# Spacing the indirect DMAs of a gated scan with a mixture-of-experts layer by waits on TensorE's products

## The chip, the core and the metric

The kernel runs on one core of a Trainium2 chip. A time is the device time of one execution in microseconds (us). The number to predict is the median over several timed executions, which run without the profiler; the profile is one separate execution with the hardware profiler switched on.

## What is computed

The input x has 16 sequences of 256 tokens with 128 channels, 4096 tokens in all. Two layers follow each other, each with a residual:

```
x = x + layernorm(scan(layernorm(x)))       # gated linear recurrence along each sequence
x = x + layernorm(moe(layernorm(x)))        # 32 experts, 4 of them for each token

scan:  i = sigmoid(x Wi + bi);  r = sigmoid(x Wr + br)
       a = exp(-8 softplus(cap) r);  h_t = a_t h_(t-1) + sqrt(1 - a_t^2) i_t x_t
moe:   s = sigmoid(x gate_w^T);  the 4 highest of s + e_bias, weights s normalised over the 4
       out = sum over the 4 of  w * ( (silu(x w1[e]) * (x w3[e])) w2[e] )       # 128 -> 96 -> 128
```

The reference computes all 32 experts for every token and multiplies the unchosen ones by zero.

## The kernel before

The 4096 tokens are cut into eight chunks of 512 tokens. For every chunk, `mix(c)` does the scan layer, the second layernorm and the router. After that a chunk goes one of two ways.

**Two dense chunks (0 and 7).** All 32 experts are computed for all of their tokens, in 24 steps per chunk. A step (`dense`) is two products into the hidden width (`dg` and `du`, line 990), a product that spreads the router weights (`dw`, line 990), an activation (line 998), two multiplications on VectorE (lines 1001 and 1007), and a product that accumulates the output (`acc`, line 1011). These steps depend on no DMA once the weights are in, so they can be run wherever TensorE has nothing else to do.

**Six routed chunks, in two groups (1, 2, 3) and (4, 5, 6).** Their tokens are sorted by expert through DRAM:

1. `send` writes each token's row into `rows_in`, at a place within its expert's rows: 16 indirect DMAs per chunk (4 row tiles of 128 tokens by 4 choices), issued by GpSimd (POOL), line 450.
2. `loads` reads blocks of 128 rows of one expert back (`xb`, line 790), after all 48 sends of the group. SyncE (SP) issues them.
3. `experts` works on tiles of four such blocks, 20 tiles per group: transposes, the `gu` products (line 820), silu and a multiplication, transposes, and the `y_ps` products (line 850). The result goes to `rows_out` in DRAM (line 861).
4. `fetch` reads each token's four results back, 16 indirect DMAs per chunk, line 928, after all the stores of the group. VectorE weighs and adds them (lines 936, 940, 944).
5. `combine` does the last layernorm and the residual and stores the chunk.

POOL issues 192 indirect DMAs and, after the first 20 us, nothing else.

**The order of the work** is not left to queues. The kernel has a planner, the class `Order`, which runs while the program is built. Every piece of work (`mix`, `send`, `dense` and so on) is a generator that yields steps such as `yield PE, 0.86`: an engine, and the time that the step is taken to need. The planner keeps the time at which each engine comes free, always takes the step that can begin first, and among steps of one engine that can begin within 0.3 us of each other the one with the earliest due time. The code behind a `yield` is issued at once when its step is chosen. So the order of the instructions in each engine's queue is the order of the planned beginnings, with all engines interleaved in one sequence. On the chip only data dependences hold, and each engine takes its queue in order. The planned times themselves do not reach the chip.

The planned steps that matter here are a send or fetch of one row tile, `yield POOL, 1.29 * K` (K is 4, so 5.16 us for four DMAs), and those of the products: 0.86 us for `dg`, `du` and `acc`, 0.22 us for `dw`, `0.33 * m` for m blocks of `gu` and `0.22 * nb` for nb blocks of `y_ps`. Dense steps have the latest due times for TensorE (400 and more), so they are taken when nothing else is ready.

Of the kernel before, what the change touches and what calls it, by code (L numbers as in the profile page):

```python
# [18 lines left out]
P = 128  # L19
EPS = 1e-5  # L20
K = 4
GROUPS = ((1, 2, 3), (4, 5, 6))
DENSE = (0, 7)
MIXES = 6
TILES = 40
HELD = 4
# [2 lines left out]
PE, DVE, ACT, POOL, SP, TIME = "pe", "dve", "act", "pool", "sp", "time"  # L29
# [88 lines left out]
SOON = 0.3  # L118
STAY = 6.0
LEAD, STEP, PACE = 45.0, 20.6, 0.9  # L120
SLOT, UNTIL = "slot", "until"


@with_exitstack
def tile_gated_scan_then_moe(
# [28 lines left out]
    nc = tc.nc  # L154
# [6 lines left out]
    SEQS = CH // T  # L161
    NG = len(GROUPS)
    TG = [CH * len(chunks) for chunks in GROUPS]
    UB = E * I // P
    NB = [t * K // P + E - 1 for t in TG]
    NBM = max(NB)
    QB = 4
    RB = 3
    assert C == P and H == P and CH % T == 0 and E * I % P == 0 and 3 * E <= P
    assert sorted(sum(GROUPS, ()) + DENSE) == list(range(N // CH))  # L170

# [20 lines left out]
    def after(ins, others):  # L192

        for o in others:
            tc.add_manual_dep(
                ins.ins, o.ins.name,
                mybir.DependencyInfo(mybir.DependencyClass.Sync, mybir.DependencyReason.DATA),
                reason="rows in DRAM",
            )
# [225 lines left out]
    def apart(ins, key):  # L425

        tc.declare_no_dep(ins.ins, group=key, reason="rows of their own")
        tc.add_to_no_dep_group(key, ins.ins)
# [7 lines left out]
    def normalize(comb, pool, c):  # L436
# [2 lines left out]
        nc.vector.reciprocal(total, total)  # L439
        nc.vector.tensor_tensor(comb, comb, total.to_broadcast([P, TPC, E]), ALU.mult)  # L440

    def send(g, cg):

        c = GROUPS[g][cg]
        yield UNTIL, lambda: times["rows", c][0] if ("rows", c) in times else None
        _, rows, hn = times["rows", c]
        for j in range(TPC):
            yield POOL, 1.29 * K
            for k in range(K):
                ins = nc.gpsimd.indirect_dma_start(  # L450
                    out=rows_in[g],
                    out_offset=bass.IndirectOffsetOnAxis(ap=rows[:, j, k : k + 1], axis=0),
                    in_=hn[:, j, :], in_offset=None,
                )
                apart(ins, f"in_{g}")
                sent[g].append(ins)
        times["sent", g] = order.now
        yield TIME, 2.5
        give("hn", "w")
# [25 lines left out]
    def mix(c):  # L485

        g = next((g for g in range(NG) if c in GROUPS[g]), None)
        if g is not None:
            cg = GROUPS[g].index(c)
        yield UNTIL, lambda: 0.0 if c < MIXES else times.get(("mixed", c - MIXES))  # L490
# [266 lines left out]
    ended = [0] * NG  # L757
# [36 lines left out]
    def experts(g, q):  # L794

        nb, n_ = min(QB, NB[g] - q), f"{g}_{q}"
        yield UNTIL, lambda: times["xb", g, q][0] if ("xb", g, q) in times else None
        yield UNTIL, lambda: 0.0 if began[g] == q // QB else None
        yield SLOT, "blk", "w", "w", "w"
        began[g] += 1  # L800
        _, xb = times["xb", g, q]
        yield SLOT, "s", "ps"
        yield PE, 0.11 * nb
        pt = bank(f"xT_ps_{n_}")
        for b in range(nb):
            nc.tensor.transpose(pt[:, b * P : (b + 1) * P], xb[:, b, :], ident)  # L806
        give("xb", "w")
        yield ACT, 0.6
        xT = work.tile([P, QB * P], F32, tag="w", name=f"xT_{n_}")
        nc.scalar.copy(xT[:, : nb * P], pt[:, : nb * P])  # L810
        give("s", "ps")
        act = work.tile([P, QB, P], F32, tag="w", name=f"act_{n_}")[:, :, :I]
        for h in range(0, nb, 2):
            m = min(2, nb - h)
            yield SLOT, "s", "ps"
            yield PE, 0.33 * m
            pg = bank(f"gu_{n_}_{h}")[:, : 4 * I].rearrange("p (b f) -> p b f", b=2)
            for b in range(m):
                _, e = regs[g, q + h + b]
                nc.tensor.matmul(  # L820
                    pg[:, b, :], lhsT=xT[:, (h + b) * P : (h + b + 1) * P],
                    rhs=w13[:, :, bass.ds(e, 1), :].rearrange("h s o i -> h s (o i)"),
                    start=True, stop=True,
                )
            yield ACT, 0.33, "silu"
            nc.scalar.activation(act[:, h : h + m, :], pg[:, :m, 0:I], AF.Silu)  # L826
            yield DVE, 0.35
            nc.vector.tensor_tensor(  # L828
                act[:, h : h + m, :], act[:, h : h + m, :], pg[:, :m, I : 2 * I], ALU.mult
            )  # L830
            give("s", "ps")
        yield SLOT, "s", "ps"
        yield PE, 0.11 * nb
        pa = bank(f"aT_ps_{n_}")
        for b in range(nb):
            nc.tensor.transpose(pa[:I, b * P : (b + 1) * P], act[:, b, :], ident)  # L836
        aT = work.tile([P, QB * P], F32, tag="w", name=f"aT_{n_}")[:I]
        if q // QB % 2:
            yield DVE, 0.6
            nc.vector.tensor_copy(aT[:, : nb * P], pa[:I, : nb * P])  # L840
        else:
            yield ACT, 0.6
            nc.scalar.copy(aT[:, : nb * P], pa[:I, : nb * P])  # L843
        give("s", "ps")
        yield SLOT, "s", "ps"
        yield PE, 0.22 * nb
        py = bank(f"y_ps_{n_}").rearrange("p (b h) -> p b h", h=H)
        for b in range(nb):
            _, e = regs[g, q + b]
            nc.tensor.matmul(  # L850
                py[:, b, :], lhsT=aT[:, b * P : (b + 1) * P],
                rhs=w2_sb[:, bass.ds(e, 1), :].rearrange("i o h -> i (o h)"),
                start=True, stop=True,
            )
        yield SLOT, "yb", "w"
        yield ACT, 0.6
        yb = work.tile([P, QB, H], F32, tag="w", name=f"yb_{n_}")
        nc.scalar.copy(yb[:, :nb, :], py[:, :nb, :])  # L858
        give("s", "ps", "blk", "w", "w", "w")
        yield SP, 0.4  # L860
        done[g].append(nc.sync.dma_start(
            out=rows_out[g].rearrange("(i p) h -> p i h", p=P)[:, q : q + nb, :],
            in_=yb[:, :nb, :],
        ))
        ended[g] += 1
        if (q // QB + 1) % RB == 0 or q + QB >= NB[g]:
            give("regs")
        times["done", g] = order.now
        yield TIME, 2.5
        give("yb", "w")  # L870
# [46 lines left out]
    def fetch(g, cg, j):  # L917

        c = GROUPS[g][cg]
        yield UNTIL, lambda: times["done", g] + 2.5 if ended[g] * QB >= NB[g] else None  # L920
        yield UNTIL, lambda: times["slots", c][0] if ("slots", c) in times else None
        yield UNTIL, lambda: 0.0 if fetched[0] == turn[c] * TPC + j else None
        yield SLOT, "yk", "w"
        _, rows, wk = times["slots", c]
        yield POOL, 1.29 * K
        yk = work.tile([P, K, H], F32, tag="w", name=f"yk_{c}_{j}")
        for k in range(K):
            ins = nc.gpsimd.indirect_dma_start(  # L928
                out=yk[:, k, :], out_offset=None, in_=rows_out[g],
                in_offset=bass.IndirectOffsetOnAxis(ap=rows[:, j, k : k + 1], axis=0),  # L930
            )
            after(ins, done[g])
        fetched[0] += 1
        yield TIME, 2.4
        yield DVE, 0.7
        nc.vector.tensor_tensor(
            yk, yk, wk[:, j, :].unsqueeze(2).to_broadcast([P, K, H]), ALU.mult
        )
        yield DVE, 0.7
        nc.vector.tensor_tensor(yk[:, 0:2, :], yk[:, 0:2, :], yk[:, 2:4, :], ALU.add)  # L940
        yield UNTIL, lambda: times["res", c][0] if ("res", c) in times else None
        yield DVE, 0.4
        ff = times["res", c][1]
        nc.vector.tensor_tensor(ff[:, j, :], yk[:, 0, :], yk[:, 1, :], ALU.add)
        give("yk", "w")
        summed[c] = summed.get(c, 0) + 1
        times["summed", c] = order.now
# [19 lines left out]
    accs, acts = {}, {}  # L967
    downs = [0] * len(DENSE)

    def dense(d, k):  # L970

        c = DENSE[d]
        yield UNTIL, lambda: times["hT", c][0] if ("hT", c) in times else None
# [13 lines left out]

        def product(name, lhsT, rhs):
            ps = bank(f"d{name}_{c}_{k}")
            nc.tensor.matmul(ps, lhsT=lhsT, rhs=rhs, start=True, stop=True)  # L990
            return ps

        yield PE, 0.86
# [24 lines left out]
    def finish(d):  # L1018

        c = DENSE[d]  # L1020
        yield UNTIL, lambda: times["down", d] if downs[d] == UB else None
# [31 lines left out]
    for g, chunks in enumerate(GROUPS):  # L1053
# [15 lines left out]
        ]  # L1069
    for d, c in enumerate(DENSE):  # L1070
        pieces += [
# [36 lines left out]
```

## Time and profile before

| | |
|---|---|
| timed executions | 440.73 us median of 3 (436.21 to 441.47) |
| profiled execution | 580.8 us, of which the span from first to last instruction is 579.1 us |
| mean granted TensorE clock in the profile | 0.823 |
| TensorE (PE) busy | 368.5 us, 64% of the span |
| VectorE (DVE) busy | 313.5 us, 54% |
| ScalarE (ACT) busy | 251.6 us, 43% |
| GpSimd (POOL) busy | 202.9 us, 35% |
| sends (line 450) | 96 indirect DMAs, 92.7 us busy, 965 ns each |
| fetches (line 928) | 96 indirect DMAs, 93.1 us busy, 970 ns each |
| first send, last send begins | 78.62 us, 293.99 us |
| first fetch, first fetch of the second group, last fetch begins | 331.98 us, 463.43 us, 522.52 us |

A row of the timeline gives the start, the duration, the engine, the line, the operation and the tiles, then in brackets the idle time of the engine before the row and what ended it. PEld is the loading of weights into TensorE. "remote" and "another core or an unknown queue" stand where the trace shows no event that ended a wait; "issue" is time in which the engine waited for nothing that the trace shows. The profiled execution took 580.8 us and the timed ones 440.73 us, so a time read from the profile is not on the scale of the timed runs, and a reader has to say each time which of the two is meant.

### The profile page before, as it was taken

What the parts mean: (1) busy time and instruction counts of PE and PEld (TensorE: products, weight loads), DVE (VectorE), ACT (ScalarE), POOL (GpSimd) and SP (SyncE); (2) the same over time, 40 slices, a digit from 0 to 9 for tenths busy, and PEclk for the clock granted to TensorE, in tenths of its full rate; (3) what the DMA queues carried; (4) which work ended last, traced back from release to release, by engine and by line L of the source; (5) the groups of instructions that cost most, each with busy time, mean ns of one, the idle gap of its engine ahead of it and who ended that gap; (6) DMA issues with size and microseconds to landing.
All of it is one profiled execution on the core that took longest, in us unless ns stands there. A gap on an engine that the chain in (4) does not pass through costs nothing.

```text
span 579.1 us, 6527 instructions
## 1 busy us (share of the span) xinstructions
PE 368.5 (64%) x1555; PEld 236.8 (41%) x1555; DVE 313.5 (54%) x1185; ACT 251.6 (43%) x473; POOL 202.9 (35%) x227
## 2 busy tenths in 40 slices
PE   0345766767883982588559863288799993235940
PEld 0123342332432871477447542266678631012410
DVE  6956692839482763287218640257577451013785
ACT  1599895659421741666235311144355520001321
POOL 9200046643645017100720077236400077771000
PEclk9986767779698887699759985599899998666995
DMA  8245535100131133223222432044544212110001
GB/s 236 66 133 140 139 91 152 41 32 25 50 100 64 55 101 100 73 70 109 91 70 59 119 109 71 25 120 132 146 118 139 88 45 54 53 51 14 18 1 54
DMA packets 82068, 48.57 MB, mean 84 GB/s; under 512 B 15696, under 2 KB 78960, under 8 KB 82032
## 3 DMA queue, kind: packets, MB, share of 16 engines
q1 hardware_dynamic: 74976, 35.40, 21.6%
q0 software_dynamic: 6144, 12.60, 7.5%
q10 hardware_dynamic: 912, 0.17, 0.2%
q8 instruction: 13, 0.21, 0.1%
q14 instruction: 23, 0.19, 0.1%
HBM read 25.20 MB, written 22.94 MB: 83 GB/s over the span
## 4 chain that ended last, share of the span: by engine, by line
PE 48%; another core or an unknown queue 16%; DVE 13%; ACT 11%; issue 11%; DMA 1%; ACTq 0%; DVEq 0%
PE gu L820 9%; PE acc L1011 8%; PE y_ps L850 7%; PE dg L990 6%; PE du L990 6%; PE aT_ps L836 3%; PE xT_ps L806 2%; PE pl L569 2%; PE dw L990 1%; PE pi L510 1%; PE pr L510 1%; ACT h L395 1%; DVE nt_a L375 1%; DVE st_a L471 1%
## 5 line engine op out<-in xcount | busy, mean ns | idle before, releaser
L450 POOL DMA_INDIRECT rows_in<-hn,rows x96 | 92.7, 965 | 184.3 <-DVE x_all L551 60.6
L928 POOL DMA_INDIRECT yk<-rows_out,slots x96 | 93.1, 970 | 135.4 <-PE dw L990 50.1
L820 PE MATMUL gu<-w,xT 128*128 x316 | 71.3, 360 | 36.9 <-ACT xT L810 19.0
L1011 PE MATMUL acc<-a,w_all 128*128 128x512 f32 x96 | 58.4, 698 | 48.2 <-DVE a L1007 28.5
L820 PEld LDWEIGHTS gu<-w,xT 128*128 128x128 f32 x316 | 56.8, 210 | 45.9 <-issue 23.3
L998 ACT ACTIVATE a<-dg 128x512 f32<-128x512 f32 x48 | 28.6, 598 | 92.8 <-remote 38.6
L1007 DVE TENSOR_TENSOR a<-a,dw 128x512 f32<-128x512 f32 x48 | 32.4, 684 | 64.3 <-remote 34.9
L850 PE MATMUL y_ps<-w_sb,aT 96*128 x316 | 48.7, 305 | 26.2 <-ACT aT L843 11.3
L828 DVE TENSOR_TENSOR act<-act,gu 128x192 f32<-128x192 f32 x80 | 27.0, 346 | 67.9 <-ACT act L826 53.1
L850 PEld LDWEIGHTS y_ps<-w_sb,aT 96*128 96x128 f32 x316 | 43.8, 212 | 39.9 <-ACT aT L843 16.3
L826 ACT ACTIVATE act<-gu 128x192 f32<-128x192 f32 x80 | 25.7, 330 | 68.7 <-PE gu L820 29.7
L990 PE MATMUL dg<-hT,w 128*128 128x512 f32 x96 | 55.4, 662 | 0.0
L990 PE MATMUL du<-hT,w 128*128 128x512 f32 x96 | 50.9, 612 | 0.0
L858 ACT COPY yb<-y_ps 128x512 f32<-128x512 f32 (+1 forms) x40 | 23.1, 581 | 52.5 <-PE y_ps L850 23.4
L1001 DVE TENSOR_TENSOR a<-a,du 128x512 f32<-128x512 f32 x48 | 32.4, 681 | 23.6 <-issue 7.4
L1011 PEld LDWEIGHTS acc<-a,w_all 128*128 128x128 f32 x96 | 17.0, 211 | 67.9 <-DVE a L1007 40.3
L810 ACT COPY xT<-xT_ps 128x512 f32<-128x512 f32 (+1 forms) x40 | 22.8, 582 | 33.5 <-remote 23.8
L836 PE MATMUL aT_ps<-ident,act 128*96 128x128 f32 x158 | 25.6, 287 | 11.1 <-issue 7.4
L990 PEld LDWEIGHTS dg<-hT,w 128*128 128x128 f32 x96 | 20.2, 217 | 19.0 <-issue 17.6
L836 PEld LDWEIGHTS aT_ps<-ident,act 128*96 128x96 f32 x158 | 18.5, 132 | 19.4 <-issue 15.5
L806 PE MATMUL xT_ps<-ident,xb 128*128 128x128 f32 x158 | 25.4, 297 | 0.4 <-DVE lists L749 0.4
L990 PEld LDWEIGHTS du<-hT,w 128*128 128x128 f32 x96 | 18.7, 205 | 14.6 <-issue 13.0
(205 smaller groups left out, 590.2 us busy)
## 6 DMA issues: line engine op xcount, KB each, us to landing
xb<-rows_in SPq DMA_DIRECT2D x158, 64.0 KB
rows_out<-yb SPq DMA_DIRECT2D x38, 256.0 KB
rows_in<-zeros SPq DMA_DIRECT2D x8, 512.0 KB
w<-in_L_ffn_w_dram SPq DMA_DIRECT2D x8, 384.0 KB
x_all<-in_L_attn_x_dram SPq DMA_DIRECT2D x8, 256.0 KB
w_all<-in_L_ffn_w_dram SPq DMA_DIRECT2D x4, 384.0 KB
w_sb<-in_L_ffn_w_dram SPq DMA_DIRECT2D x4, 384.0 KB
rows_in<-hn,rows POOLq DMA_INDIRECT x96
```

What stands on the lines that cost most here:

```text
L450: ins = nc.gpsimd.indirect_dma_start(out=rows_in[g], out_offset=bass.IndirectOffsetOnAxis(ap=rows[:, j, k : k + 1], axis=0), in_=hn[:, j, ...
L806: nc.tensor.transpose(pt[:, b * P : (b + 1) * P], xb[:, b, :], ident)
L820: nc.tensor.matmul(pg[:, b, :], lhsT=xT[:, (h + b) * P : (h + b + 1) * P], rhs=w13[:, :, bass.ds(e, 1), :].rearrange("h s o i -> h s (o i) ...
L828: nc.vector.tensor_tensor(act[:, h : h + m, :], act[:, h : h + m, :], pg[:, :m, I : 2 * I], ALU.mult)
L836: nc.tensor.transpose(pa[:I, b * P : (b + 1) * P], act[:, b, :], ident)
L850: nc.tensor.matmul(py[:, b, :], lhsT=aT[:, b * P : (b + 1) * P], rhs=w2_sb[:, bass.ds(e, 1), :].rearrange("i o h -> i (o h)"), start=True, ...
L928: ins = nc.gpsimd.indirect_dma_start(out=yk[:, k, :], out_offset=None, in_=rows_out[g], in_offset=bass.IndirectOffsetOnAxis(ap=rows[:, j, ...
L990: nc.tensor.matmul(ps, lhsT=lhsT, rhs=rhs, start=True, stop=True)
L998: nc.scalar.activation(a, pg, AF.Silu)
L1001: nc.vector.tensor_tensor(a, a, pu, ALU.mult)
L1007: nc.vector.tensor_tensor(a, a, pw, ALU.mult)
L1011: nc.tensor.matmul(accs[d], lhsT=w2_all[:, k, :], rhs=a, start=(k == 0), stop=(k == UB - 1))
```

## The change

Three things are changed, all for the indirect DMAs.

- Each send, and each fetch that is issued while `left()` holds, waits for `beat[0]`: the last product that was issued ahead of it in the one planned sequence. Such products are `y_ps` (line 850) of the experts, and `dg`, `du` and `dw` (line 990) of the dense chunks.
- In the planner each indirect DMA has a slot of its own of `RATE`, 1.9 us, where four together had 5.16 us (1.29 us each).
- `left()` is true until both dense chunks have issued all 24 steps and all expert tiles of both groups have ended, in the planned sequence. Fetches issued after that have a slot of 1.26 us and no wait.

```diff
+RATE = 1.9
...
+    beat = [None]
+
+    def in_pace(ins):
+
+        if beat[0] is not None:
+            after(ins, beat)
+
+    def left():
+
+        return sum(downs) < len(DENSE) * UB or any(ended[g] * QB < NB[g] for g in range(NG))
+
     def send(g, cg):
...
         for j in range(TPC):
-            yield POOL, 1.29 * K
             for k in range(K):
+                yield POOL, RATE
                 ins = nc.gpsimd.indirect_dma_start(
...
                 apart(ins, f"in_{g}")
+                in_pace(ins)
                 sent[g].append(ins)
...
-            nc.tensor.matmul(
+            beat[0] = nc.tensor.matmul(
                 py[:, b, :], lhsT=aT[:, b * P : (b + 1) * P],
...
         _, rows, wk = times["slots", c]
-        yield POOL, 1.29 * K
         yk = work.tile([P, K, H], F32, tag="w", name=f"yk_{c}_{j}")
         for k in range(K):
+            yield POOL, RATE if left() else 1.26
             ins = nc.gpsimd.indirect_dma_start(
...
             after(ins, done[g])
+            if left():
+                in_pace(ins)
...
         def product(name, lhsT, rhs):
             ps = bank(f"d{name}_{c}_{k}")
-            nc.tensor.matmul(ps, lhsT=lhsT, rhs=rhs, start=True, stop=True)
+            beat[0] = nc.tensor.matmul(ps, lhsT=lhsT, rhs=rhs, start=True, stop=True)
             return ps
```

`after(ins, others)` adds a dependence: `ins` waits for the semaphores of `others`. `downs[d]` counts the dense steps whose `acc` has been issued, `ended[g]` the expert tiles of a group whose store has been issued. UB is 24, QB is 4 and NB is 79 blocks per group.

More of the change, by code (lines that the diff above doesn't have):

```diff
@@ L21 @@
 K = 4
-GROUPS = ((1, 2, 3), (4, 5, 6))
-DENSE = (0, 7)
+GROUPS = ((1,2,3),(4,5,6))
+DENSE = (0,7)
 MIXES = 6
```

## The prediction

> **What bounds the kernel now.** I read the page first, then the timeline of POOL alone, the timeline of all engines over the last 120 us, the table by stretches, and the chain of waits.
>
> ```profile
> span 579.1 us, 6527 instructions
> ...
> PE 48%; another core or an unknown queue 16%; DVE 13%; ACT 11%; issue 11%; DMA 1%; ACTq 0%; DVEq 0%
> ...
> L450 POOL DMA_INDIRECT rows_in<-hn,rows x96 | 92.7, 965 | 184.3 <-DVE x_all L551 60.6
> L928 POOL DMA_INDIRECT yk<-rows_out,slots x96 | 93.1, 970 | 135.4 <-PE dw L990 50.1
> ```
>
> The chain that ends last runs 48% over PE, but 27% of it (16 + 11, about 153 us of 579.1) is time that no event explains. The timeline of the last stage shows where such time lies:
>
> ```profile
> 468.90 1.12 PE L1011 MATMUL acc<-a,w_all 128*128 128x512 f32 x2
> ...
> 471.89 1.13 PE L1011 MATMUL acc<-a,w_all 128*128 128x512 f32 x2
> ...
> 505.17 0.60 ACT L998 ACTIVATE a<-dg 128x512 f32<-128x512 f32 x1 [18.37 <-remote]
> ...
> 509.31 0.69 DVE L1007 TENSOR_TENSOR a<-a,dw 128x512 f32<-128x512 f32 x1 [13.38 <-remote]
> ...
> 522.52 0.94 POOL L928 DMA_INDIRECT yk<-rows_out,slots  x1 [0.30 <-issue]
> ```
>
> A dense step takes 2.99 us (from one acc to the next) until 480 us. Then ACT sits idle for 18.37 us although its product was ready, while POOL issues fetches 1.25 us apart. By stretches:
>
> ```profile
> 440.00:463.00 23.00, 22.68 (x126) 16.92 (x125) 13.65 (x42) 12.08 (x28) 0.00 (x0) 1.00 0.34 99
> 463.00:480.00 17.00, 15.86 (x38) 5.95 (x37) 9.46 (x16) 2.99 (x5) 12.60 (x14) 1.00 0.17 46
> 480.00:529.00 49.00, 12.88 (x21) 4.89 (x20) 5.51 (x10) 1.79 (x3) 33.11 (x35) 0.64 0.18 48
> 529.00:560.00 31.00, 27.33 (x65) 10.66 (x63) 23.57 (x73) 6.90 (x13) 0.00 (x0) 0.96 0.03 9
> ```
>
> (stretch; length; busy time of PE, PEld, DVE, ACT, POOL; granted clock; DMA share; GB/s.) PE is full before the last run of fetches, 26% busy in the middle of it, full after it. So the profiled run is slowed by whatever stops PE, ACT and DVE some ten DMAs into a run of indirect DMAs, and spacing these DMAs out looks like the cure.
>
> **But the timed runs do not contain most of those stalls.** 580.8 - 440.73 = 140 us is missing from them, and the unexplained part of the chain is 153 us: 13 us would be left. The chain's PE part, 48% or 278 us at a clock of 0.82, may shrink by some 28 us at a fuller clock (0.92, an estimate: the table above has 1.00 outside the runs of fetches), which would leave up to 41 us. So stalls in the timed runs are worth 0 to 41 us; I take near 0, because the last stage alone fits it, as follows. Fetch of the last 48 rows: 463.43 to 523.46, 60.0 us. After it, without stalls: landing about 2 us (estimate from the 2.4 us that the planner leaves), DVE 1.4 us (L936, L940, L944), and from the last layernorm's start at 570.14 to the end 9.0 us: together 12.4 us. Timed: 440.73 - 1.7 (outside the span) - 12.4 - 60.0 = 366.6 us as the start of this run of fetches, against 463.43 in the profile. Of the 140 us, 43 lie behind that point and 97 before it.
>
> What then bounds a timed run is **PE until the experts end at about 364 us, then POOL**: 48 fetches by 1.25 us, solid, while PE does the dense steps left. I count 18 acc pairs after 463 us: 18 x 2.98 = 54 us, hidden in the 60.
>
> [...] The rows of the tile yk:
>
> ```profile
> L928 POOL DMA_INDIRECT yk<-rows_out,slots x96: 939/945/1806, 332.0 to 522.5; - x96
> L936 DVE TENSOR_TENSOR yk<-yk,wk x24: 678/684/748, 373.5 to 568.8; 128x512 f32<-128x512 f32 x24
> ```
>
> Minimum, median and maximum in ns: the multiplication with both inputs in SBUF takes 684 ns inside the runs and outside. All 96 fetches together exceed their median by 93.1 - 96 x 0.945 = 2.4 us. [...]
>
> **The change, part by part.**
>
> *The waits themselves.* 96 sends and at least part of the fetches get a semaphore wait on PE. The nearest row is a waiting instruction on DVE's queue, 21 ns; the spread is 0 to 0.3 us each (the gap that POOL has anyway). I take nothing: POOL is paced by PE, not by this. Nothing but later indirect DMAs is queued behind them on POOL. But SP's loads wait for all sends of a group, with the experts' stores behind them in SP's queue; and DVE's sums (L936 on) wait for fetches, with dense multiplications behind them.
>
> *The sends.* A chunk's 16 sends get 16 x 1.9 = 30.4 us where they had 20.6. Since the products keep the planned order, POOL can no longer run ahead of it. The three chunks of group 0 began at 78.62, 103.75 and 137.52 us and ended at 157.5; taking out the unexplained entries of the chain there (2.6 and 4.1 at 94, 5.1 at 118, 2.2 at 153: 14 us) that is about 143.5. With the slots, back to back: 78.6 + 91.2 = 170. **The experts of group 0 begin 26 us later** (12 if no stall is taken out). PE doesn't have to wait: the dense steps of chunk 0 are there, eight at 2.98 us. DVE, 1.4 us per step beside the routers' work, was the busier engine there; I take five, 15 us. The other 11 us go mostly to the scan work of chunks 5 to 7, drawn forward (some 7 us of PE a chunk, by the share of the first 78 us): 2 us of PE lost, ends 0 and 11. What is late next is group 1: its 48 sends end another 91 us later, while group 0's experts fill PE.
>
> *The fetches of group 0.* 48 x 1.9 = 91 us of slots among expert tiles. There PE is slower than its slots: 8 `y_ps` blocks take 1.16 us against 0.88, `gu` 1.56 against 1.32. At some 1.2 times the slots the fetches take about 109 us, and group 1's experts about 97 (profile: 131 us from 332 to 463, less the 34 of unexplained entries). So POOL comes free up to 12 us after the experts end, in which PE does up to four dense steps; I take the middle, two.
>
> *The dense work is moved.* Five and two steps done earlier leave R = 18 - 7 = 11 behind the start of the last fetches. PE's total is the same, so those fetches start 7 x 2.98 + 2 = **23 us later**, at 389.5.
>
> *The last 48 fetches.* While dense steps are left, a fetch gets 1.9 us of slots, in which a step has 2.8 us (3 x 0.86 + 0.22) and takes 2.98: 2.02 us real. 11 x 2.98 = 32.8 us hold 16.2 fetches; the other 31.8 run at 1.25: 39.8 us. Sum 72.5 against 60.0: **12.5 us more**. Nothing hides it, for this stage is POOL's.
>
> Sum: 23 + 12.5 = +35.4, **476 us timed**. In general it is 53.6 - 1.84 R + L (L is lost PE time): R = 18, L = 0 gives +20; R = 8, L = 11 gives +50. A step moved forward costs, since the work left beside the fetches is what hides them.
>
> *In the profiled execution's own time* the same +35 stands against stalls that should shrink: at 2 us and more between DMAs I guess half to three quarters of the 140, so 580.8 + 35 - 88 = about 528 us. **The profile may become faster while the timed runs become slower.**
>
> **Rivals.**
>
> - *The stalls are in the timed runs* (up to 41 us) and spacing removes them. For it: they hang on back-to-back DMAs. Against it: the 140 us. With R = 18: 440.7 + 20 - 41 = 420. It is 2% faster (432 us) from 29 us of stalls upwards at R = 18, from 44 at R = 11, which is more than the bound. Chance 0.08.
> - *No measurable change* (432 to 450): 25 to 35 us of stalls go and pay for the pace, or the slots do not bind. 445 us, 0.08.
> - *Only the tail pays*: the front delay is covered without dense work (R = 18), 461 us, 0.24. Speaks for it: experts have earlier due times than dense steps and might catch up.
> - *PE starves* between the old and the new start of the experts, and again before group 1: L = 12 to 30, 490 to 505 us, 0.17. Speaks for it: DVE 71% busy in the first 78 us, so dense steps may be too slow to fill.
> - The forecast, 466 to 488 around 476: 0.43.
>
> **How the numbers follow.** Faster 0.08, within 2% 0.08, slower 0.84; 2% is about what a measurement of this kernel can tell from no change (its three runs lie 1.2% apart). The range 450 to 500 leaves out the faster case, most of no change and the far end of starvation. The likeliest case's own range is 466 to 488.
>
> **What would show it.** Right: sends and fetches about 2 us or more apart, released by products of L850 and L990, with 30 us for a chunk; `xb` loads of group 0 later among the dense steps; about 11 acc pairs after group 1's first fetch; that run of 48 fetches over 70 us long; fewer long waits put down to "remote". Wrong: 18 or more acc pairs left there with the fetches still 60 us (the slots do not bind), or a timed median below 440 (the stalls were real). If the timed runs are slower with more stalls in the profile, my reading of the stalls is wrong.

## The result, and the profile after

The timed executions after the change have a median of **478.51 us** (477.88 to 480.04, 4 runs), those of before beside them 439.39 us (436.21 to 441.47, 4 runs). The ratio is 1.090, with a 95% interval of 1.082 to 1.098: the change costs 39 us.

The profiled execution of after took 477.88 us; it is one of these four. From its page, the span, the chain and the two groups of indirect DMAs (count, busy us, mean ns of one, then the idle time of POOL before them and what ended most of it):

```profile
span 476.2 us, 6622 instructions
...
PE 50%; ACT 16%; DVE 14%; issue 10%; POOL 6%; DMA 3%; POOLq 0%; ACTq 0%; SPq 0%; DVEq 0%
...
L462 POOL DMA_INDIRECT rows_in<-hn,rows x96 | 95.4, 994 | 162.5 <-ACT xn L511 61.5
L941 POOL DMA_INDIRECT yk<-rows_out,slots x96 | 93.1, 969 | 95.1 <-PE y_ps L863 20.4
```

Two things are to be seen. The part "another core or an unknown queue", 16% of the chain before, is gone. And a fetch costs POOL what it cost before (969 ns, 970 before); what has changed is when it begins.

The profile shown ahead of the prediction took 580.8 us where timed executions took 440. So the kernel before was profiled again, unchanged. From the page of this second profile:

```profile
span 437.1 us, 6527 instructions
...
PE 58%; ACT 16%; DVE 14%; issue 5%; DMA 3%; POOL 2%; SPq 1%; ACTq 0%; POOLq 0%; DVEq 0%
...
L928 POOL DMA_INDIRECT yk<-rows_out,slots x96 | 94.6, 985 | 83.3 <-PE dw L990 34.0
```

It took 438.82 us and has no such entry. Of the 39 later timed executions of before (434.55 to 442.48 us) none was slow in this way either. All comparisons of traces below are with this second profile.

The first trace is not only slow but incomplete. It holds 5514 updates of semaphores, the second trace of the same kernel 9252, those of all other kernels 9234 to 9356. So it has no landing time for any fetch, where the second one has a median of 2.9 us:

```profile
yk<-rows_out,slots POOLq DMA_INDIRECT x96
```

```profile
yk<-rows_out,slots POOLq DMA_INDIRECT x96, 2.9
```

A wait is called "remote" or put down to an unknown queue where no update is found that ended it. Part of these entries is therefore missing records. The standstill itself is real: all instructions are recorded, and their span is 579.1 us.

**Where the 39 us lie.** The last stage of before by stretches (stretch; length; busy time of PE, PEld, DVE, ACT, POOL; granted clock; DMA share; GB/s), cut where the last 48 fetches begin and where the last dense step ends:

```profile
341.00:364.00 23.00, 22.80 (x126) 16.64 (x124) 13.72 (x43) 11.74 (x27) 0.29 (x1) 1.00 0.32 94
364.00:414.00 50.00, 48.88 (x116) 19.07 (x115) 36.02 (x83) 11.32 (x21) 38.12 (x40) 1.00 0.21 55
414.00:425.00 11.00, 0.66 (x4) 0.42 (x4) 8.91 (x42) 3.52 (x9) 8.46 (x9) 0.60 0.38 97
```

The same of after:

```profile
370.00:393.00 23.00, 22.98 (x119) 16.05 (x118) 13.84 (x30) 9.60 (x21) 11.69 (x13) 1.00 0.41 112
393.00:425.00 32.00, 31.22 (x75) 12.13 (x73) 21.94 (x53) 7.50 (x14) 15.95 (x17) 1.00 0.15 42
425.00:464.00 39.00, 0.90 (x5) 0.42 (x4) 21.53 (x81) 5.38 (x13) 29.83 (x31) 0.57 0.28 73
```

Before, PE still had 50 us of dense work when the last fetches began at 363.71, and 40 of the 48 were issued beside it; POOL went on without PE for 11 us. After, the last fetches begin at 392.91, only 32 us of dense work are left, and only 18 fetches are issued beside it; POOL goes on without it for 39 us. The last fetch is issued 12 us before the end in both. So the 39.1 us between the two spans are

- 29.2 us: the last fetches begin later (363.7 to 392.9), and
- 10.0 us: they take longer (61.2 to 71.2).

The later start splits without remainder, by arithmetic; what causes the two parts is for the experiments to show. It is how much later the last dense step ends (413.7 to 425.2, **11.5 us**: PE time lost) plus how much less dense work is left behind the start (50.0 to 32.3, **17.7 us**: dense work drawn forward). This split is used for every kernel below, each from one profiled execution. The timed executions of before lie up to 8 us apart, so a few us in it can be chance.

### The profile page after: what moved, and what is told of

It reads as the page before. It is cut to its first block, busy times and chain, and to the rows that moved or that the text cites. A ratio compares the mean times of both kernels' runs of the same rounds, so it can differ in the third digit from the quotient of the medians.

```text
span 476.2 us, 6622 instructions
## 1 busy us (share of the span) xinstructions
PE 342.0 (72%) x1555; PEld 220.8 (46%) x1555; DVE 316.2 (66%) x1185; ACT 252.3 (53%) x473; POOL 205.7 (43%) x227
## 4 chain that ended last, share of the span: by engine, by line
PE 50%; ACT 16%; DVE 14%; issue 10%; POOL 6%; DMA 3%; POOLq 0%; ACTq 0%; SPq 0%; DVEq 0%
PE gu L833 10%; PE acc L1026 7%; PE y_ps L863 7%; PE dg L1005 6%; PE du L1005 6%; POOL yk L941 6%; PE aT_ps L849 3%; PE xT_ps L819 3%; DMA yk<-rows_out,slots 2%; ACT h L396 2%; PE dw L1005 2%; ACT hn L396 1%; ACT L542 1%; ACT L534 1%; PE pl L582 1%
## 5 line engine op out<-in xcount | busy, mean ns | idle before, releaser
L462 POOL DMA_INDIRECT rows_in<-hn,rows x96 | 95.4, 994 | 162.5 <-ACT xn L511 61.5
L833 PE MATMUL gu<-w,xT 128*128 x316 | 67.0, 348 | 13.4 <-issue 11.9
L833 PEld LDWEIGHTS gu<-w,xT 128*128 128x128 f32 x316 | 54.4, 202 | 24.1 <-issue 13.7
L1026 PE MATMUL acc<-a,w_all 128*128 128x512 f32 x96 | 53.6, 647 | 7.1 <-DVE a L1022 6.5
L841 DVE TENSOR_TENSOR act<-act,gu 128x192 f32<-128x192 f32 x80 | 26.9, 348 | 43.9 <-ACT act L839 43.7
L1005 PE MATMUL dg<-hT,w 128*128 128x512 f32 x96 | 50.0, 602 | 0.0
L863 PE MATMUL y_ps<-w_sb,aT 96*128 x316 | 43.7, 285 | 3.0 <-ACT act L839 1.0
L863 PEld LDWEIGHTS y_ps<-w_sb,aT 96*128 96x128 f32 x316 | 39.4, 195 | 13.0 <-ACT aT L856 4.2
L1016 DVE TENSOR_TENSOR a<-a,du 128x512 f32<-128x512 f32 x48 | 32.3, 681 | 6.1 <-PE du L1005 3.9
L396 ACT ACTIVATE ff<-ff,sh_d,rs_d 128x128 f32<-128x128 f32 x24 | 9.9, 482 | 36.6 <-DVE sh_d L393 36.6
L849 PE MATMUL aT_ps<-ident,act 128*96 128x128 f32 x158 | 24.4, 281 | 6.0 <-issue 4.7
L951 DVE TENSOR_TENSOR yk<-yk,wk 128x512 f32<-128x512 f32 x24 | 16.5, 688 | 17.4 <-DMA yk<-rows_out,slots 17.3
L1005 PEld LDWEIGHTS du<-hT,w 128*128 128x128 f32 x96 | 17.9, 196 | 17.0 <-issue 12.9
```

The lines of the kernel that those rows point to most:

```text
L462: ins = nc.gpsimd.indirect_dma_start(out=rows_in[g], out_offset=bass.IndirectOffsetOnAxis(ap=rows[:, j, k : k + 1], axis=0), in_=hn[:, j, ...
L833: nc.tensor.matmul(pg[:, b, :], lhsT=xT[:, (h + b) * P : (h + b + 1) * P], rhs=w13[:, :, bass.ds(e, 1), :].rearrange("h s o i -> h s (o i) ...
L841: nc.vector.tensor_tensor(act[:, h : h + m, :], act[:, h : h + m, :], pg[:, :m, I : 2 * I], ALU.mult)
L863: beat[0] = nc.tensor.matmul(py[:, b, :], lhsT=aT[:, b * P : (b + 1) * P], rhs=w2_sb[:, bass.ds(e, 1), :].rearrange("i o h -> i (o h)"), s ...
L1005: beat[0] = nc.tensor.matmul(ps, lhsT=lhsT, rhs=rhs, start=True, stop=True)
L1016: nc.vector.tensor_tensor(a, a, pu, ALU.mult)
```

## The experiments

The first question was what in the 580.8 us belonged to the kernel; then which of the three edits (waits, slots, pace of the last fetches) costs what; then sends against fetches; at last where the lost PE time comes from.

**The kernel before, profiled again** (no edit).

> The kernel before, unchanged, profiled a second time. Theory A (the stalls belong to the recording of the profile, not to the kernel): the profile shows long runs of back-to-back indirect DMAs with PE, ACT and DVE standing still again, and takes well over 500 us (about 580), while its timed runs stay at 436 to 442 us. Rival B (the stalls are a rare state of the chip or of one execution, not tied to recording): the profiled execution takes about 440 us, with hardly any wait put down to 'remote', the last 48 fetches begin near 367 us, and 18 dense steps are left behind that point.

Measured: 438.82 us, no stalls. The 140 us were neither in the timed executions nor in this second profile. What stopped three engines in that one execution is open; no later execution showed it. A disturbance of the recording is not excluded, since that trace lacks four in ten of its semaphore updates. On its timeline the last fetches begin and go like this:

```profile
363.71 0.94 POOL L928 DMA_INDIRECT yk<-rows_out,slots  x1 [33.08 <-PE dw L990]
364.96 0.94 POOL L928 DMA_INDIRECT yk<-rows_out,slots  x1 [0.30 <-issue]
...
423.94 0.95 POOL L928 DMA_INDIRECT yk<-rows_out,slots  x1 [0.30 <-issue]
```

That is the solid run of 48 at 1.25 us that the prediction placed at 366.6.

**The slots without the waits.**

```diff
     def in_pace(ins):
 
-        if beat[0] is not None:
-            after(ins, beat)
+        return
```

> The change without its waits: the slots of 1.9 us in the planned order stay, so every engine has the order of the changed kernel, but POOL is free to issue each indirect DMA as soon as its data are there. Theory A (order and pace): the last fetches still begin at about 392 us, since the experts end where the order puts them, but run at 1.25 us each, 60 us instead of 71: about 466 us, 12 less than the changed kernel, 27 more than before. Rival (the waits are the whole cost): 440 us. Rival (the DMAs' contention matters in timed runs): no faster than the changed kernel, 478 us or more.

Measured: 468.43 us, ratio 1.067 (1.055 to 1.079). The start of the last fetches is where it is with the waits (392.9). The run of fetches is 62.7 us, 8.5 less than with the waits and 1.5 more than before: without the waits POOL goes nearly as fast as in before.

**The waits without the slots.** The plan again takes 1.29 us for each DMA, four by four.

```diff
-                yield POOL, RATE
+            yield POOL, 1.29 * K
...
-            yield POOL, RATE if left() else 1.26
+        yield POOL, 1.29 * K
```

> The kernel before with the waits of the change on sends and fetches, but the old slots of 5.16 us for four DMAs. The order of all engines is that of before. Theory A: POOL is held to PE's progress. The start of the last fetches stays at about 367 us; while 18 dense steps run at 2.98 us, where the slots assume 2.8, a fetch takes 1.37 us: 39 fetches in 54 us, the other nine at 1.25, 65 us instead of 60. 442 to 447 us. Rival (the waits are the whole cost of the change): 470 us or more. Rival (each wait itself costs some 0.1 to 0.3 us on POOL): 450 to 455 us.

Measured: 442.47 us, ratio 1.007 (1.003 to 1.010). The waits on all sends and most fetches cost 3 us together by this ratio, since the plan that they wait for is that of before. In the traces the start of the last fetches moves by 2.0 us and their run is 2.3 us longer.

**The last 48 fetches without slot and wait**, all else as after.

```diff
-            yield POOL, RATE if left() else 1.26
+            yield POOL, RATE if g == 0 else 1.26
...
-            if left():
+            if g == 0:
                 in_pace(ins)
```

> The changed kernel, with the fetches of the second group at 1.26 us slots and without waits from the first on; sends and the first group's fetches as changed. Theory A: the last fetches begin at about 392 us as in the changed kernel and take 60 us: about 466 us. If the start moves too, the two costs (start and length) are not separate as the prediction has them. Rival (the loss lies before the experts' end alone): 478 us.

Measured: 468.53 us, ratio 1.070 (1.060 to 1.080), 10.0 us less than after. The timeline of POOL shows the run solid from its first DMA, at the start that after has:

```profile
393.11 0.94 POOL L941 DMA_INDIRECT yk<-rows_out,slots  x1 [0.30 <-issue]
```

Against it the same place of after, where 12 of the first 18 DMAs begin after a longer gap than 0.30 us, most of them released by a product of a dense step:

```profile
392.91 0.94 POOL L941 DMA_INDIRECT yk<-rows_out,slots  x1 [0.99 <-PE du L1005]
395.03 0.94 POOL L941 DMA_INDIRECT yk<-rows_out,slots  x1 [1.18 <-PE dw L1005]
397.79 0.94 POOL L941 DMA_INDIRECT yk<-rows_out,slots  x1 [1.82 <-PE dw L1005]
399.04 0.94 POOL L941 DMA_INDIRECT yk<-rows_out,slots  x1 [0.30 <-issue]
401.63 0.94 POOL L941 DMA_INDIRECT yk<-rows_out,slots  x1 [1.65 <-PE dw L1005]
...
461.94 0.94 POOL L941 DMA_INDIRECT yk<-rows_out,slots  x1 [0.30 <-issue]
463.19 0.94 POOL L941 DMA_INDIRECT yk<-rows_out,slots  x1 [0.30 <-issue]
```

**Only the sends paced**, fetches as before.

```diff
-            yield POOL, RATE if left() else 1.26
+        yield POOL, 1.29 * K
...
-            if left():
-                in_pace(ins)
```

> All 96 sends with slots of 1.9 us and waits, all fetches as before. Unlike with the first group's sends alone, POOL's queue keeps the sends chunk by chunk. Theory A: the first expert tile begins at about 177 us as in the changed kernel (151 before), without a wait of PE for xb; about 15 dense steps are left behind the start of the last fetches; that start is at about 384 us and the run 61 us: 459 us, 13 less than the 473.5 of the mixed order. Rival (the 473.5 are the price of the late first group itself): 470 us or more.

Measured: 461.43 us, ratio 1.050 (1.043 to 1.057). Start of the last fetches +22.8, of which 13.2 are lost PE time and 9.7 drawn-forward dense work; their run is as before, 61.2 us.

**Only the sends of the first group paced.** As the last, and in `send`:

```diff
-                yield POOL, RATE
+                yield POOL, RATE if g == 0 else 1.29
...
-                in_pace(ins)
+                if g == 0:
+                    in_pace(ins)
```

> Only the 48 sends of the first group have the slots of 1.9 us and the waits; the second group's sends have 1.29 us each and no wait, all fetches are as before. Theory A (the front delay is where the start of the last fetches moves, partly by dense steps drawn forward, partly by lost PE time): the first expert tile begins some 25 us later; about 15 dense steps are left behind the start of the last fetches, where before has 18, and PE's last acc comes some 10 us later than before's 414. So the last fetches begin at about 383 us, run 61 us, and the time is about 458 us. Rival (PE fills the whole front delay with dense steps, nothing lost): last acc at 414, last fetches begin at about 373, 448 us. Rival (the delay is caught up by the time the experts end): 441 us.

Measured: 473.54 us, ratio 1.076 (1.067 to 1.085), worse than with all sends paced. The run doesn't answer its question, because the order of POOL's queue was no longer the planned one. The kernel pins the order of PE, DVE, ACT and SP as it was planned, and not that of POOL:

```
tc.manual_schedule(engines={ET.PE, ET.DVE, ET.Activation, ET.SP})
```

With waits on some sends and none on others, the builder put sends of chunks 4 and 5, which wait for no product, ahead of those of chunk 3. POOL's queue by chunk, after the sends of chunks 1 and 2 (this list is not from the profile, whose views do not tell the chunks apart):

```
3 x2, 4 x2, 3, 4 x2, 3, 4, 3 x3, 4 x10, 3, 4, 3 x7, 5 x4, 3, 5 x12, 6 x16
```

(In after, and with all sends paced, each chunk's 16 stand together.) By this list the last send of the first group, the one all its loads wait for, is the 68th of the queue and not the 48th. The trace agrees: the 48th send begins at 162.8 us and the 68th at 188.9, and the first load follows at 191.5. The timeline of PE shows the price:

```profile
193.43 0.47 PE L820 MATMUL xT_ps<-ident,xb 128*128 128x128 f32 x1 [13.27 <-DMA xb<-rows_in]
```

**Only the fetches of the first group paced.** Sends as before, and the edit of the run with free last fetches:

```diff
-                yield POOL, RATE
+            yield POOL, 1.29 * K
...
-                in_pace(ins)
...
-            yield POOL, RATE if left() else 1.26
+            yield POOL, RATE if g == 0 else 1.26
...
-            if left():
+            if g == 0:
                 in_pace(ins)
```

> Only the first group's 48 fetches have slots of 1.9 us and waits; all sends are as before, the second group's fetches have 1.26 us and no wait. Theory A: POOL is not free when the second group's experts could end, dense steps fill PE meanwhile, and no PE time is lost: about 14 dense steps left instead of 18, last acc still at 414 us, last fetches begin at about 376 and run 61 us: 451 us. Rival (these fetches have room among the experts and cost nothing): 439 to 442 us.

Measured: 453.44 us, ratio 1.029 (1.022 to 1.036). The first group's fetches end at 370.0 instead of 330.6 and the last ones begin 11.4 us later; 10.2 of these are drawn-forward dense work and 1.2 lost PE time.

**All fetches paced, the sends not.** The fetches are those of after:

```diff
-                yield POOL, RATE
+            yield POOL, 1.29 * K
...
-                in_pace(ins)
```

> All sends as before, all fetches as in the changed kernel. Theory A: the last fetches begin at about 376 us as with the first group's fetches alone, and the 14 dense steps left hold some 20 fetches at 2 us, the rest at 1.25: about 74 us instead of 61, so 464 us. With the formula of the prediction, more steps left make the run of fetches longer than the changed kernel's 71 us. Rival (the run of fetches has the same 71 us whatever is left): 461 us, not separable; rival (no cost without the sends): 440 us.

Measured: 465.44 us, ratio 1.055 (1.047 to 1.063). The run of the last fetches is 73.2 us here, 12.0 longer than before.

**A slot of 1.5 us**, all else as after.

```diff
-RATE = 1.9
+RATE = 1.5
```

> The changed kernel with RATE 1.5 instead of 1.9. Theory A: about 15 dense steps are left at the start of the last fetches, which begins at about 374 us, and 28 of the 48 fetches run at 1.6 us, the rest at 1.25: 69 us. About 457 us, near half of the way between before and the changed kernel. Rival (a threshold: below some spacing the DMAs collide and the time goes up again): 478 us or more. Rival (spacing helps up to a point): below 439 us.

Measured: 466.52 us, ratio 1.059 (1.052 to 1.067), 9.5 us above the expectation. The run of the last fetches is the 69 us expected (68.7), but it begins at 383.2 instead of 374: the expectation had hardly any lost PE time, and 9.5 us were lost. At the two slots tried the price grows with the slot: 5.9% at 1.5 us, 9.0% at 1.9.

**Chunk 7 prepared earlier**, on after. In after the dense steps of chunk 0 are used up at 221 us and those of chunk 7 begin at 280, since its router comes late; between them PE has no dense step to fill with:

```profile
221.36 1.91 PE L1026 MATMUL acc<-a,w_all 128*128 128x512 f32 x2
...
280.06 1.02 PE L1026 MATMUL acc<-a,w_all 128*128 128x512 f32 x2
```

Was this pause of 59 us the cause of the lost PE time?

```diff
-    pieces = [(LEAD + STEP * c, mix(c)) for c in range(N // CH)]
+    pieces = [(LEAD + STEP * (c if c < 7 else 4.5), mix(c)) for c in range(N // CH)]
```

> The changed kernel, with the scan and router work of dense chunk 7 due earlier (as if it were chunk 4.5), so that its dense steps are there when chunk 0 has no more. Theory A: in the changed kernel chunk 0's steps are used up at 221 us and chunk 7's begin at 280, which leaves PE with gaps: the lost PE time. Here the pause is shorter and the last acc comes earlier, by some 7 us (418 instead of 425), but the steps are only drawn forward: 8 or fewer are left behind the start of the last fetches, the start does not get earlier, and the time stays at 476 to 482 us. Rival (the lost PE time is what the change costs): 470 us or less.

Measured: 484.33 us, ratio 1.103 (1.095 to 1.111). The pause became 36 us (208 to 244), and the last dense step ended at 425.2 as in after, not at 418. So a shorter pause did not make the loss smaller. But the stretch in which PE is least full moved with it. PE's stretches (columns as above, PE's busy time first):

```profile
200.00:240.00 40.00, 32.62 (x210) 27.53 (x211) 27.04 (x119) 20.64 (x45) 16.49 (x17) 0.95 0.40 119
240.00:280.00 40.00, 37.69 (x210) 29.04 (x209) 28.27 (x96) 18.27 (x41) 14.81 (x15) 0.92 0.44 126
```

After has 35.2 and 33.5 us there, before 36.3 and 35.7. From 280 to 360, where few dense steps are left, PE is busy for 69.2 us with chunk 7 earlier, 70.7 in after and 73.3 before. And 30.0 us of dense work were drawn forward instead of 17.7, the last fetches began at 405.3, and the kernel became slower, with the same lost PE time: drawing dense work forward is what cost the rest.

**Dense work held back**, the opposite direction, on before: the second dense chunk may not begin until the expert tiles of the second group have all begun.

```diff
+        if d == 1 and k >= 0:
+            yield UNTIL, lambda: 0.0 if began[1] * QB >= NB[1] else None
```

> The kernel before, with one line more: no dense step of chunk 7 begins, in the planned order, until the last expert tile of the second group has begun. It is the opposite of the change: steps are moved behind the start of the last fetches, which have room for some 20. Theory A: 21 or 22 steps are left there instead of 18; the start of the last fetches comes 4 to 5 us earlier (359 instead of 364), the run of fetches stays 61 us, the last acc comes some 6 us later (420), still hidden: 434 to 437 us against 439. Rival (PE needs these steps as filler among the experts, and the experts don't get faster): 440 us or more.

Measured: 446.74 us, ratio 1.016 (1.011 to 1.021): slower, where I expected a gain. 21 dense steps instead of 18 were left, 12.1 us more work behind the start; but 16.3 us of PE time were lost on the way. Nor was this work still hidden: the last dense step ended at 430.0 us, after the last fetch had been issued (428.7), and the chunk's last layernorm then took VectorE ahead of the last sums. The last fetch is 18.6 us before the end here, 12.2 in before. These 6.4 us and the 4.2 of the later start make up the 10.2 us between the two traces. The stretch of expert tiles, first of before, then of this kernel (columns as above, PE's busy time first):

```profile
280.00:320.00 40.00, 34.84 (x218) 27.60 (x217) 28.34 (x90) 21.23 (x48) 30.78 (x31) 1.00 0.63 164
```

```profile
280.00:320.00 40.00, 30.79 (x179) 26.23 (x177) 24.96 (x82) 19.24 (x44) 30.56 (x32) 0.87 0.59 158
```

So dense steps seem to have two uses: to fill PE among the expert tiles, and to do work beside the last fetches, where it costs no time. Before spends them better than either of these two kernels; none of the kernels tried was faster than before.

All traces split in the same way (us against the second profile of before; "drawn forward" is dense work that is no longer behind the start of the last fetches, and the first two columns add up to the later start; only with dense work held back is there a fourth part, the 6.4 us behind the last fetch):

| kernel | PE time lost | dense work drawn forward | longer run of the last 48 fetches |
|---|---|---|---|
| after | 11.5 | 17.7 | 10.0 |
| slots without waits | 13.2 | 16.0 | 1.5 |
| waits without slots | 1.6 | 0.4 | 2.3 |
| last fetches free | 11.8 | 17.6 | -0.1 |
| sends only | 13.2 | 9.7 | 0.0 |
| sends of the first group only (order mixed) | 22.8 | 9.7 | 0.5 |
| fetches of the first group only | 1.2 | 10.2 | -0.1 |
| all fetches only | 3.4 | 11.7 | 12.0 |
| slot of 1.5 us | 9.5 | 10.0 | 7.5 |
| chunk 7 earlier | 11.5 | 30.0 | 3.6 |
| dense work held back | 16.3 | -12.1 | -0.4 |

Among the parts of the change the first column belongs to the slots of the sends: it is 13.2 with the sends alone, and at most 3.4 where the sends keep their old slots. It is not theirs alone, though: moving dense work without any change of the sends, as in the last row, lost 16.3.

## Why the prediction was right, and where not

The forecast, 476 us for 478.5, stood on the right mechanism: POOL's last run sets the end, the slots push dense work out of its cover, and the pace makes the run longer. Step by step:

- **"The timed runs do not contain most of those stalls"**: right, they hold none that a trace shows, so spacing had nothing to cure. What caused the stalls is another matter. Profiling did not bring them again: the same kernel took 438.82 us in its second profile and ran without them. Whether the recording was disturbed in that one execution is open; its missing updates speak for it, but not for which came first. They also mean that the 27% of the chain "that no event explains" was in part time whose events were not recorded. That the profile of after would take about 528 us is wrong: it took 477.88. I had treated one odd execution as a property of profiles.
- **The state of before** was reconstructed well: last fetches at 366.6 (363.7 in the second profile), 18 dense steps behind it (18), a run of 60.0 (61.2), an estimated clock of 0.92 (0.921), an estimated landing of about 2 us (2.5, the median of the 12 of these fetches whose landing the second profile has). One sum is off without consequence: 278 us at 0.92 instead of 0.82 shrink by 30 us, not 28.
- **The rows of the tile `yk`**, where the multiplication with both inputs in SBUF took the same 684 ns beside the fetches and without them, were borne out. Its median is 684 ns in both profiles of before and 688 after the spacing, which had nothing to gain there:

```profile
L951 DVE TENSOR_TENSOR yk<-yk,wk x24: 676/688/693, 303.9 to 465.8; 128x512 f32<-128x512 f32 x24
```

- **The waits themselves**, "nothing": 3 us for all of them, nearly right.
- **The sends**: 30.4 us for a chunk and an end at 170. Measured: the three chunks took 27, 31 and 29 us and ended at 168.0; the first transpose of the experts moved from 150.8 to 177.0 us, 26.2 for the 26 forecast. But "I take five", with DVE as the limit, was too few: seven dense steps more than before had begun when the first expert product came, and PE was as full as before in this stretch (34.2 of 40 us from 140 to 180, 34.0 before).
- **The fetches of the first group**: forecast 109 us, measured 99.0 (292.9 to 391.9). POOL came free 4 us after the experts' end at 387.9, inside the 0 to 12 given.
- **"R = 18 - 7 = 11"**: 11 to 12 were left, though not as five and two (the seven ahead of the experts made up all of it), or 17.7 us of work drawn forward where 7 steps of 2.98 us had been put, 20.9.
- **The lost PE time, taken as 2 us, is the term that was mis-sized: 11.5 us**, at the far end of the 0 to 11 given. Its place was wrong too. I looked for it while PE waits for the late experts; there seven dense steps filled it. It lies later, among the expert tiles. From the pages, PE's rows of before and after (the total, then the `gu` products):

```profile
PE 337.0 (77%) x1555; PEld 216.6 (50%) x1555; DVE 314.8 (72%) x1185; ACT 251.8 (58%) x473; POOL 205.4 (47%) x227
...
L820 PE MATMUL gu<-w,xT 128*128 x316 | 65.0, 338 | 7.5 <-issue 6.7
```

```profile
PE 342.0 (72%) x1555; PEld 220.8 (46%) x1555; DVE 316.2 (66%) x1185; ACT 252.3 (53%) x473; POOL 205.7 (43%) x227
...
L833 PE MATMUL gu<-w,xT 128*128 x316 | 67.0, 348 | 13.4 <-issue 11.9
```

The same 1555 products take 5.0 us longer, and the rest of the 11.5, 6.5 us, is idle time; ahead of the `gu` products the idle time grew by 5.9. By stretches, the slower products lie where the clock was lower, before and then after:

```profile
200.00:240.00 40.00, 36.31 (x238) 30.10 (x236) 27.17 (x116) 25.28 (x56) 10.59 (x12) 0.96 0.38 110
240.00:280.00 40.00, 35.73 (x206) 26.67 (x206) 28.93 (x100) 18.74 (x40) 14.23 (x15) 1.00 0.43 121
```

```profile
200.00:240.00 40.00, 35.22 (x181) 26.98 (x182) 23.32 (x113) 18.62 (x40) 13.71 (x15) 0.79 0.33 99
240.00:280.00 40.00, 33.50 (x228) 29.99 (x227) 29.70 (x106) 23.00 (x49) 16.45 (x17) 0.96 0.49 142
```

The same transposes of 128x128 (`xT_ps`) take 328 ns on average from 200 to 240 us in after (median 273, up to 473), and 274 before (273, up to 307). Why the clock was lower there is open.

That the slots of the sends bring this loss is shown. How they do is only in part. In three kernels PE is less busy in a stretch within the pause of the dense steps than before in the same stretch: 33.5 us for 35.7 in after (240 to 280), 32.6 for 36.3 with chunk 7 earlier (200 to 240), 30.8 for 34.8 with dense work held back (280 to 320). So it seems that PE goes idle where it has no dense step to fill with. But the total did not shrink with the pause, most of the idle time has no event that explains it ("issue"), and with chunk 7 earlier the idle time ahead of `gu` was only 4.3 us while the total loss stayed the same.

- **The last 48 fetches**: forecast 12.5 us more, with 2.02 us for each while dense steps last. Measured 10.0 more; 17 gaps from 392.91 to 425.02 make 1.89 us each, the slot itself. The run with the last fetches free puts the same 10.0 us on this edit.

So 20.9 + 2 + 12.5 was 35.4, and 17.7 + 11.5 + 10.0 is 39.2: two terms were some 3 us too large, and one 9.5 us too small. That the time came out 2.5 us from the forecast is therefore partly luck: errors of opposite sign cancelled. The formula for the sum, with R = 11.5 and L = 11.5, gives 43.9, so its price of a dense step was a little too high.

The rivals: real stalls (420 us) and no change (445) fell with the 478.51 us themselves, and the second profile shows no stalls that could go. "Only the tail pays" needed R = 18, and about 11.5 were left. "PE starves" had a loss of 12 to 30 us; 11.5 came, just short of that, but later than this rival had it, among the expert tiles.

## What to carry to other kernels

Before a profile is used to find a stall, its own time is set against the timed executions, and its records are checked for gaps; a stall that the timed executions cannot hold is nothing to cure. Where a serial queue sets the end and other work is hidden behind it, the work left at that queue's last start is the number to watch: widening the slots upstream used it up early here, and what was moved forward was missed at the end. And an order that is pinned for some engines only can change on the others, as POOL's did here once some of its sends had a wait and others none: read the queue before reading the time.

## What the runs showed of the hardware

- One execution of before took 580.8 us, with ACT, DVE and PE stopped together during runs of indirect DMAs (from 480 to 529 us PE is busy for 12.9, DVE for 5.5, ACT for 1.8); the same kernel profiled again took 438.82. The cause is open.
- Spacing did not help these DMAs. The time from issue to landing of the last 48 fetches, before (1.25 us apart) and then after (1.89 us apart at first), minimum, median and maximum, as far as the traces know it (12 and 24 of the 48):

```profile
DMA to landing us min/median/max: 2.5/2.5/3.0
```

```profile
DMA to landing us min/median/max: 2.4/2.6/4.0
```

So a solid run of 48 shows no queue building up behind POOL: the median gains nothing from the spacing, and POOL's own 0.94 us and the gap of 0.30 make the 1.25 us from one to the next. (The 2.9 us above is the median over both groups; it is 3.0 for those of the first, which run among the expert tiles.)
- Each engine took its queue in order. In the first profile of before, and in that of after, the rows follow each other by line as in the program's own queues: PE changes line 347 and 342 times, DVE 847 and 830, ACT 267 and 270, each time where the program does, and so do the 238 DMAs that SP issues and the 192 of POOL. The planned times did not hold POOL back: with slots of 1.9 us and no waits the last 48 fetches took 62.7 us, 1.31 each.
